# Scan layer of a four-layer convolution network: dt summed on TensorE, one PSUM tile for both banks, wider state rows

## The chip, the cores and the metric

One core of a Trainium2 chip runs the whole program in one launch. The metric is the device time of an execution in microseconds (us). The engines are named as in the profile: PE is TensorE (PEld its weight loads), DVE is VectorE, ACT is ScalarE, POOL is GpSimd, SP is SyncE, which here only issues DMAs. Each engine works through its own queue in order and waits for the others by semaphores.

## What is computed

Four layers, each with a residual: attention blocks on a 3 x 256 x 48 x 48 input, a convolution with weights mixed per image, a plain convolution, and a state-space scan over the 2304 positions of each image. Only the scan layer is touched. Its core in the reference:

```
u = silu(causal_conv(x_in))                       # 512 channels
dt = softplus(dt_raw @ dt_proj_w.T + dt_proj_b)   # 512 channels
def step(hst, inp):
    dt_t, B_t, C_t, u_t = inp
    dA = exp(dt_t[:, :, None] * A)
    hst = hst * dA + dt_t[:, :, None] * B_t[:, None, :] * u_t[:, :, None]
    y_t = einsum('bdn,bn->bd', hst, C_t)          # 16 states per channel
    return hst, y_t
y = (ys + u * D_param) * silu(z)
out = einsum('bld,cd->blc', y, out_proj_w)
```

softplus(p) is computed as max(p, 0) + ln(1 + exp(-|p|)).

## The kernel before

The scan layer cuts each image into 6 chunks of 384 positions, so there are 18 chunks. A chunk has 8 steps (`s`): 4 groups of 128 channels (`m`) times 2 halves of the 16 states (`h`). A step holds a state tile `hs` of 128 partitions x 2 x 4 rows; a row holds one starting state and 384 positions, so 385 columns. Three buffers of `hs` and two of the product `hc` rotate.

In each step:

- `fill` (L1711 on DVE, L1715 on POOL) writes dt·u·B into `hs`, half of the rows by each engine; it is issued one step ahead.
- `decay` (L1740, ACT) writes exp(dt·A) of one row into one of three PSUM slots `ps_da`. It is issued three rows ahead, and a slot is free again when the scan of three rows earlier has ended.
- `scan` (L1748, DVE) runs the recurrence along one row in place. There are 8 per step ("row 0" to "row 7" here).
- `times_c` (L1765, POOL) multiplies the finished tile by C; `add_states` (L1777, L1782, PE) sums the states into `ps_y`; every second step `gate` (L1789, DVE) multiplies by silu(z).

Beside the scans of a chunk, the next chunk is prepared in two PSUM banks, `bank[0]` and `bank[1]` (`ps_g`), which are two tiles. The list `plan` (with `after` and `gating`) fixes where: an entry has a half step `j` (0 to 15, two to a step) and a place in it. MID comes after the second row of the half step, DONE after the third, LATE after the fourth, and PE_ after the fourth too (for odd `j` at the end of the step). `keep_order` makes the order of PE, DVE, ACT and POOL exactly that of the code. The entries that matter:

- `taps` (L1264, PE, j = 0, 1, 3, 4): the causal convolution of one channel group into bank m % 2; `take_u` (L1273, ACT, MID of j = 2, 3, 5, 6) copies each out.
- `project_y` (L1353 and L1355, PE, j = 5 and 6) and `store` (L1365, ACT): the layer's output of the chunk before, in bank 0 and then bank 1.
- `silu` of u (ACT, LATE of j = 7), `project_u` (L1284, PE), `take_dbc` (L1292, ACT, LATE of j = 8), `project_dt` (L1310, PE, j = 8 and 10): the projection p for two channel groups at a time, one per bank.
- `softplus` (ACT, LATE of j = 9 and 11): |p| from each bank (L1319), then exp (L1320) and ln (L1321) on both.
- `take_dt` (DVE, MID of j = 10 and 12): L1326 adds max(p, 0) to the logarithm in the bank, L1327 multiplies dt by u; twice, once per bank.
- `keep_dt` (L1331, ACT, DONE of j = 10 and 12): copies dt out of both banks; DMAs then write dt and dt·u to DRAM, from where `spread` loads them again with each channel repeated.
- `less_mean` (L1222, PE, j = 12), `centre` (L1235 to L1237, ACT), `square_mean` (L1229, PE), `inverse_root` (L1241, L1242, ACT, MID of j = 14), `normalise` (L1246, DVE, MID of j = 15): the layer norm of the chunk after next.
- `project_z` (L1341, PE, j = 13, 14, 15) and `take_z` (L1349, ACT): the gate's input.

Chunk 0 is prepared by `early_preparation` beside the convolution before. In the profile's names, `x`, `u` and `sz` stand for rooms cut out of tiles of other layers that are free by then (dt is one of them), and `wconv` for a piece of a buffer of weights that is free by then.

Of the kernel before, what the change touches and what calls it, by code (L numbers as in the profile page):

```python
# [9 lines left out]
F32 = mybir.dt.float32  # L10
I32 = mybir.dt.int32
AF = mybir.ActivationFunctionType
ALU = mybir.AluOpType
# [3 lines left out]
P = 128  # L17
# [3 lines left out]
CT = 2  # L21
# [4 lines left out]
CH = 384  # L26
# [10 lines left out]
DS = 16  # L37
DTR = 16
DCONV = 4


SUM_MIN, SUM_MAX = 1e-18, 1e18
# [41 lines left out]
def net(  # L84
# [21 lines left out]
    nc = tc.nc  # L106
# [1096 lines left out]
        pass  # L1203


    bank = [psg.tile([P, 512], F32, name=f"ps_g{j}")[:, :CH] for j in range(2)]

# [21 lines left out]
            )  # L1231

    def centre(k):
        for ct in range(CT):
            nc.scalar.copy(k.xg[:, ct, :], bank[ct])  # L1235
        k.sq = room(k, "sq")
        nc.scalar.activation(k.sq, k.xg, AF.Square)  # L1237

# [68 lines left out]
    def project_dt(k, m0):  # L1307
        for j in range(2):
# [3 lines left out]
                start=True, stop=True,  # L1312
            )

    def softplus(k, m0):

        both = k.dt[:, m0 : m0 + 2, :]
        for j in range(2):
            nc.scalar.activation(k.dt[:, m0 + j, :], bank[j], AF.Abs)  # L1319
        nc.scalar.activation(both, both, AF.Exp, scale=-1.0)  # L1320
        nc.scalar.activation(both, both, AF.Ln, bias=1.0)  # L1321

    def take_dt(k, m0):
        for j in range(2):
            m, pdt = m0 + j, bank[j]
            nc.vector.scalar_tensor_tensor(pdt, pdt, 0.0, k.dt[:, m, :], ALU.max, ALU.add)  # L1326
            nc.vector.tensor_tensor(k.dtu[:, m, :], pdt, k.u[:, m, :], ALU.mult)  # L1327

    def keep_dt(k, m0):
        for j in range(2):  # L1330
            nc.scalar.copy(k.dt[:, m0 + j, :], bank[j])  # L1331
        if m0 == 0:
            k.dtd, k.dtud = {}, {}
        d = k.dtd[m0] = dram.tile([P, 2, CH], F32, name=f"dtd{m0}")
        nc.sync.dma_start(d, k.dt[:, m0 : m0 + 2, :])
        d = k.dtud[m0] = dram.tile([P // 2, 2, CH], F32, name=f"dtud{m0}")
        nc.sync.dma_start(d, k.dtu[P // 2 :, m0 : m0 + 2, :])

# [25 lines left out]
    def store(k, mo):  # L1364
# [25 lines left out]
        (7, PE_, 1, project_u),  # L1390
        (8, LATE, 1, take_dbc),
        (8, PE_, 1, lambda k: project_dt(k, 0)),
        (9, LATE, 1, lambda k: softplus(k, 0)),
        (10, MID, 1, lambda k: take_dt(k, 0)),
        (10, DONE, 1, lambda k: keep_dt(k, 0)),
        (10, PE_, 1, lambda k: project_dt(k, 2)),
        (11, LATE, 1, lambda k: softplus(k, 2)),
        (12, MID, 1, lambda k: take_dt(k, 2)),
        (12, DONE, 1, lambda k: keep_dt(k, 2)),
    ]  # L1400

    after = [
# [25 lines left out]
    def early_preparation():  # L1428

        while (2, 1) not in stored:  # L1430
            yield
        fetch(0)
        winx, cwb = x2_rooms()
        k = chunks[0]
        yield
        while 2 not in norm3:
            yield
        group_scale(k)
        yield
        for tap in (0, 1):  # L1440
            fold_taps(winx, cwb, tap)
        less_mean(k)
        yield
        centre(k)
        yield
        square_mean(k)
        yield
        for tap in (2, 3):
            fold_taps(winx, cwb, tap)
        inverse_root(k)  # L1450
        yield
        normalise(k)
        tokens(k)
        fetch(1)
        yield
        for m in (0, 1):
            taps(k, m, 0, 4)
            yield
        take_u(k, 0)
        take_u(k, 1)  # L1460
        yield
        for m in (2, 3):
            taps(k, m, 0, 4)
            yield
        take_u(k, 2)
        take_u(k, 3)
        nc.scalar.activation(k.u, k.u, AF.Silu)
        yield
        k = chunks[1]
        for stage in (group_scale, less_mean, centre, square_mean, inverse_root, normalise):  # L1470
            stage(k)
            yield
        tokens(k)
        yield

        k = chunks[0]
        while 1 not in norm3 or (1, 1) not in stored:
            yield
        x1_rooms()
        yield  # L1480
        project_u(k)
        yield
        take_dbc(k)
        yield
        for m in (0, 2):
            project_dt(k, m)
            yield
            softplus(k, m)
            yield
            take_dt(k, m)  # L1490
            yield
            keep_dt(k, m)
            yield
        for m in (0, 2):
            for j in range(2):
                project_z(k, m + j, j)
            yield
            for j in range(2):
                take_z(k, m + j, j)
            yield  # L1500
# [155 lines left out]
    with ExitStack() as l3:  # L1656
# [48 lines left out]
        def fill(s):  # L1705

            at, m, h = steps[s]
            k = chunks[at]
            hs = tiles[s]
            bb = k.bc[0][:, 2 * h : 2 * h + 2, :].unsqueeze(2).broadcast_to([P, 2, 2, CH])  # L1710
            nc.vector.tensor_tensor(  # L1711
                hs[:, :, 0:2, 1:],
                k.ps[:, :, :CH].unsqueeze(1).broadcast_to([P, 2, 2, CH]), bb, ALU.mult,
            )
            nc.gpsimd.tensor_tensor(  # L1715
                hs[:, :, 2:4, 1:],
                k.rows[m][1].unsqueeze(1).broadcast_to([P, 2, 2, CH]), bb, ALU.mult,
            )

        def first_states(s):  # L1720
            at, m, h = steps[s]
            src = zero if chunks[at].c == 0 else state[m, h]
            hs = tiles[s] = scn.tile([P, 2, 4, CH + 1], F32, name="hs", bufs=3)
            nc.scalar.copy(hs[:, :, :, 0], src.rearrange("p (g q) -> p g q", g=2))

        def last_states(s):
            at, m, h = steps[s]
            if chunks[at].c < NCH - 1:
                t = state[m, h] = wp.tile([P, 8], F32, name=f"hst{m}{h}")
                nc.scalar.copy(t.rearrange("p (g q) -> p g q", g=2), tiles[s][:, :, :, CH])  # L1730

        def decay(n):

# [10 lines left out]

        def scan(s, part):
            g, q = parts_of_step[part]
            b = tiles[s][:, g, q, :]
            nc.vector.tensor_tensor_scan(  # L1748
                b, slots[(8 * s + part) % 3][:, : CH + 1], b, 0.0, ALU.mult, ALU.add
            )  # L1750

        def times_c(s):
            at, m, h = steps[s]
            cb = chunks[at].bc[1][:, 2 * h : 2 * h + 2, :].unsqueeze(2)
            hc = scn.tile([P, 2, 4, CH], F32, name="hc")
            if s == len(steps) - 1:

                for g in range(2):
                    nc.vector.tensor_tensor(
                        hc[:, g], tiles[s][:, g, :, 1:],  # L1760
                        cb[:, g].broadcast_to([P, 4, CH]), ALU.mult,
                    )
                tiles[s] = hc
                return
            nc.gpsimd.tensor_tensor(  # L1765
                hc, tiles[s][:, :, :, 1:], cb.broadcast_to([P, 2, 4, CH]), ALU.mult
            )
            tiles[s] = hc

# [189 lines left out]
```

## Time and profile before

| what | value |
|---|---|
| time, median of 3 runs | 3457.79 us (3455.21 to 3458.74) |
| the profiled execution's own time | 3459.61 us |
| its span | 3458.2 us |
| first and last start of a scan | 2027.6 and 3436.0 us |
| DVE busy over the span | 2940.7 us (85%) |
| POOL busy over the span | 1430.7 us (41%) |
| ACT busy over the span | 2351.8 us (68%) |
| PE busy over the span | 3125.3 us (90%) |

The profile shows one execution. Its groups read "line engine operation out<-in xcount | busy us, mean ns of one | idle us before, and what ended it". In the answers in order of time a row gives start, duration, engine and line, and in brackets the idle time just before it with what ended it; equal neighbours are merged ("x16"), and then the duration is that of all together. One fp32 matmul of 384 columns appears as two records.

### The profile page before, as it was taken

How to read it: one execution, taken by the hardware profiler on the slowest of the kernel's cores; microseconds unless marked ns; L12 is line 12 of the kernel's file. 1: busy time of each engine (PE TensorE's matmuls, PEld its weight loads, DVE VectorE, ACT ScalarE, POOL GpSimd, SP SyncE). 2: the span in 40 equal slices, each digit the busy share in tenths (PEclk: the TensorE clock that was granted, in tenths of full speed). 3: DMA queues.
4: the chain of work that ended last, by engine and by line, in shares of the span. 5: the costliest groups of instructions: out<-in, count | busy, mean ns of one | idle time of the engine just before them, and what ended most of it. 6: DMA issues, size and time to landing. Idle time of an engine off the chain costs nothing.

```text
span 3458.2 us, 51943 instructions
## 1 busy us (share of the span) xinstructions
PE 3125.3 (90%) x20170; PEld 1499.8 (43%) x20170; DVE 2940.7 (85%) x3234; ACT 2351.8 (68%) x3508; POOL 1430.7 (41%) x385
## 2 busy tenths in 40 slices
PE   7999999999999999879999988888888888888885
PEld 4334343443433335447777743333343443333331
DVE  4799899859899994579965379999999999999998
ACT  3788888748888884422224457777777777777774
POOL 0000000000000001110000059999999999999997
PEclk9999999999999999989999989889999999988987
DMA  4000000010000003746402134445444444444441
GB/s 178 14 8 10 8 10 8 8 42 6 10 6 8 10 8 112 249 170 224 139 21 68 46 97 109 115 100 118 116 105 110 106 107 114 116 117 106 117 111 43
DMA packets 167603, 273.95 MB, mean 79 GB/s; under 512 B 30049, under 2 KB 134561, under 8 KB 165426
## 3 DMA queue, kind: packets, MB, share of 16 engines
q1 hardware_dynamic: 154114, 250.48, 26.9%
q10 hardware_dynamic: 13232, 20.06, 1.8%
q8 instruction: 160, 2.62, 0.3%
q14 instruction: 97, 0.79, 0.1%
HBM read 223.12 MB, written 47.10 MB: 78 GB/s over the span
## 4 chain that ended last, share of the span: by engine, by line
PE 54%; DVE 32%; ACT 8%; DMA 3%; issue 2%; POOL 0%; SPq 0%; DVEq 0%; ACTq 0%; POOLq 0%
DVE hs L1748 21%; PE ps_s L637 16%; PE acc L650 14%; PE ps_c L1513 8%; DVE hs L1711 4%; PE ps_g L1222 2%; PE ps_s L1030 2%; ACT ps_da L1740 2%; PE ps_y L461 2%; PE ps_m L664 1%; DVE u L295 1%; PE ps_m L710 1%; ACT L1278 1%; ACT L228 1%; PE acc L528 1%
## 5 line engine op out<-in xcount | busy, mean ns | idle before, releaser
L1748 DVE TENSOR_TENSOR_SCAN hs<-ps_da,hs 128x385 f32<-128x385 f32 x1152 | 1005.6, 938 | 54.4 <-ACT ps_da L1740 35.6
L641 ACT ACTIVATE pt<-ps_s 128x1024 f32<-128x1024 f32 x972 | 942.4, 1022 | 154.8 <-PE ps_s L637 142.2
L856 DVE TENSOR_TENSOR part<-part,pt 128x2048 f32<-128x2048 f32 x396 | 906.6, 2289 | 41.3 <-ACT pt L641 18.5
L1740 ACT ACTIVATE ps_da<-dtr,u 128x384 f32<-128x384 f32 x1152 | 656.0, 582 | 271.3 <-DVE hs L1748 248.4
L163 POOL TENSOR_TENSOR rstd<-ve,mhalf 128x2 f32<-128x2 f32 (+1 forms) x26 | 16.3, 629 | 1477.0 <-DVE ve L161 1477.0
L637 PE MATMUL ps_s<-q,kt 32*128 32x512 f32 (+1 forms) x4320 | 576.4, 592 | 0.1
L650 PE MATMUL acc<-pt,vt 128*32 128x512 f32 (+1 forms) x4320 | 520.9, 561 | 0.2
L1765 POOL TENSOR_TENSOR hc<-hs,x 128x3072 f32<-128x3072 f32 x72 | 446.3, 6198 | 19.8 <-DVE hs L1748 16.5
L1513 PE MATMUL ps_c<-vt,u 128*128 128x288 f32 x1728 | 433.9, 412 | 21.0 <-DVE u L262 21.0
L1765 POOL TENSOR_TENSOR hc<-hs,bc 128x3072 f32<-128x3072 f32 x71 | 438.8, 6181 | 18.6 <-DVE hs L1748 17.2
L1264 PE MATMUL ps_g<-u 128*128 128x384 f32 x1152 | 387.7, 491 | 8.2 <-ACT sz L1349 3.5
L1513 PEld LDWEIGHTS ps_c<-vt,u 128*128 128x128 f32 x1728 | 331.8, 193 | 117.8 <-issue 19.3
L1264 PEld LDWEIGHTS ps_g<-u 128*128 128x128 f32 x1152 | 214.4, 190 | 180.6 <-ACT ps_da L1740 18.7
L637 PEld LDWEIGHTS ps_s<-q,kt 32*128 32x128 f32 x4320 | 195.3, 183 | 199.1 <-issue 120.2
L1782 PE MATMUL ps_y<-hc,u 128*32 128x384 f32 x2304 | 244.8, 548 | 13.8 <-POOL hc L1765 13.8
L1715 POOL TENSOR_TENSOR hs<-dtur,x 128x1536 f32<-128x1536 f32 x72 | 248.4, 3450 | 6.9 <-DMA dtur<-dtud 6.9
L1715 POOL TENSOR_TENSOR hs<-dtur,bc 128x1536 f32<-128x1536 f32 x72 | 249.5, 3465 | 0.0
L650 PEld LDWEIGHTS acc<-pt,vt 128*32 128x32 f32 x4320 | 94.4, 108 | 353.4 <-issue 326.7
L1310 PE MATMUL ps_g<-wconv,u 17*128 17x384 f32 x144 | 79.2, 684 | 82.8 <-ACT x L1331 82.8
L1782 PEld LDWEIGHTS ps_y<-hc,u 128*32 128x32 f32 x2304 | 64.4, 117 | 172.4 <-issue 151.6
L321 POOL MEMSET xpad<- 128x212 f32 x12 | 5.6, 468 | 313.0 <-ACT xpad L1564 234.5
L1529 ACT COPY cb<-ps_c 128x288 f32<-128x288 f32 x48 | 19.2, 400 | 162.9 <-PE ps_c L1513 145.1
(246 smaller groups left out, 3685.3 us busy)
## 6 DMA issues: line engine op xcount, KB each, us to landing
wconv<-in_we SPq DMA_DIRECT2D x144, 384.0 KB, 4.3
dtr<-dtd SPq DMA_DIRECT2D x288, 192.0 KB, 3.9
dtur<-dtud SPq DMA_DIRECT2D x288, 96.0 KB, 4.2
wconv<-xd SPq DMA_DIRECT2D x36, 384.0 KB, 4.3
x<-bcd SPq DMA_DIRECT2D x72, 192.0 KB, 5.7
dtd<-x SPq DMA_DIRECT2D x36, 384.0 KB, 2.9
bc<-bcd SPq DMA_DIRECT2D x72, 192.0 KB, 6.1
yc<-ycat ACTq DMA_DIRECT2D x18, 576.0 KB, 5.0
```

What stands on the lines that cost most here:

```text
L637: nc.tensor.matmul(s[:, j, cols], kt[r, mt * P : (mt + 1) * P], q[r, :n], start=True, stop=True,)
L641: nc.scalar.activation(p[:, h0 : h0 + 2, :], s, AF.Exp)
L650: nc.tensor.matmul(acc[h * HD : (h + 1) * HD, :n], vt[:, mt, g * P + h * HD : g * P + (h + 1) * HD], p[:, h, cols], start=mt == 0, stop=mt ...
L856: ): nc.vector.tensor_tensor(part, first, p, ALU.add)
L1264: nc.tensor.matmul(bank[m % 2], w3v["wtap"][:, tap, ct, m * P : (m + 1) * P], k.xn[:, ct, tap : tap + CH], start=tap == 0 and ct == 0, sto ...
L1513: nc.tensor.matmul(pc[:, :HN], u[:, i, dy, ct, m * P : (m + 1) * P], vt[:, i, ct, dy * TW : dy * TW + HN], start=ct == 0 and dy == 0, stop ...
L1711: nc.vector.tensor_tensor(hs[:, :, 0:2, 1:], k.ps[:, :, :CH].unsqueeze(1).broadcast_to([P, 2, 2, CH]), bb, ALU.mult,)
L1715: nc.gpsimd.tensor_tensor(hs[:, :, 2:4, 1:], k.rows[m][1].unsqueeze(1).broadcast_to([P, 2, 2, CH]), bb, ALU.mult,)
L1740: nc.scalar.activation(slots[n % 3][:, 1 : CH + 1], chunks[at].rows[m][0][:, q, :], AF.Exp, scale=amat[:, col : col + 1],)
L1748: nc.vector.tensor_tensor_scan(b, slots[(8 * s + part) % 3][:, : CH + 1], b, 0.0, ALU.mult, ALU.add)
L1765: nc.gpsimd.tensor_tensor(hc, tiles[s][:, :, :, 1:], cb.broadcast_to([P, 2, 4, CH]), ALU.mult)
L1782: nc.tensor.matmul(k.y_ps[32 * q : 32 * q + 32, :CH], fold, hc[:, g, q, :], start=False, stop=h == 1 and g == 1,)
```

## The change

There are five edits, all in the scan layer.

- The two banks become two halves of one PSUM tile, `banks`; `bank[j]` is a slice of it.
- `centre`, |p| and `keep_dt` handle both banks with one instruction of 768 columns each instead of two of 384.
- |p| moves out of `softplus` to a new entry `positive_part` at MID of j = 9 and 11. The same entry writes max(p, 0) of both banks to the other half of dt's room.
- `sum_dt` at PE_ of j = 9 and 11 multiplies the positive part and the logarithm by the identity into the banks, so PE adds them. `take_dt` becomes one multiplication by u and moves from MID to DONE; `keep_dt` moves from DONE to LATE.
- A row of `hs` has 400 columns: the starting state is in column 15, and the 384 positions begin at column 16.

```diff
+ROW = 16
-    bank = [psg.tile([P, 512], F32, name=f"ps_g{j}")[:, :CH] for j in range(2)]
+    banks = psg.tile([P, 2, 512], F32, name="ps_g")[:, :, :CH]
+    bank = [banks[:, j, :] for j in range(2)]
...
     def centre(k):
-        for ct in range(CT):
-            nc.scalar.copy(k.xg[:, ct, :], bank[ct])
+        nc.scalar.copy(k.xg, banks)
...
+    def pair_of(k, m0):
+        return k.dt[:, m0 : m0 + 2, :]
+
+    def positive_part(k, m0):
+
+        nc.scalar.activation(pair_of(k, m0), banks, AF.Abs)
+        nc.scalar.activation(pair_of(k, 2 - m0), banks, AF.Relu)
+
     def softplus(k, m0):
 
-        both = k.dt[:, m0 : m0 + 2, :]
-        for j in range(2):
-            nc.scalar.activation(k.dt[:, m0 + j, :], bank[j], AF.Abs)
+        both = pair_of(k, m0)
         nc.scalar.activation(both, both, AF.Exp, scale=-1.0)
         nc.scalar.activation(both, both, AF.Ln, bias=1.0)
 
+    def sum_dt(k, m0):
+
+        for part in (2 - m0, m0):
+            for j in range(2):
+                nc.tensor.matmul(
+                    bank[j], ident, k.dt[:, part + j, :],
+                    start=part != m0, stop=part == m0,
+                )
+
     def take_dt(k, m0):
-        for j in range(2):
-            m, pdt = m0 + j, bank[j]
-            nc.vector.scalar_tensor_tensor(pdt, pdt, 0.0, k.dt[:, m, :], ALU.max, ALU.add)
-            nc.vector.tensor_tensor(k.dtu[:, m, :], pdt, k.u[:, m, :], ALU.mult)
+        nc.vector.tensor_tensor(
+            k.dtu[:, m0 : m0 + 2, :], banks, k.u[:, m0 : m0 + 2, :], ALU.mult
+        )
 
     def keep_dt(k, m0):
-        for j in range(2):
-            nc.scalar.copy(k.dt[:, m0 + j, :], bank[j])
+        nc.scalar.copy(pair_of(k, m0), banks)
...
+        (9, MID, 1, lambda k: positive_part(k, 0)),
         (9, LATE, 1, lambda k: softplus(k, 0)),
-        (10, MID, 1, lambda k: take_dt(k, 0)),
-        (10, DONE, 1, lambda k: keep_dt(k, 0)),
+        (9, PE_, 1, lambda k: sum_dt(k, 0)),
+        (10, DONE, 1, lambda k: take_dt(k, 0)),
+        (10, LATE, 1, lambda k: keep_dt(k, 0)),
         (10, PE_, 1, lambda k: project_dt(k, 2)),
+        (11, MID, 1, lambda k: positive_part(k, 2)),
         (11, LATE, 1, lambda k: softplus(k, 2)),
-        (12, MID, 1, lambda k: take_dt(k, 2)),
-        (12, DONE, 1, lambda k: keep_dt(k, 2)),
+        (11, PE_, 1, lambda k: sum_dt(k, 2)),
+        (12, DONE, 1, lambda k: take_dt(k, 2)),
+        (12, LATE, 1, lambda k: keep_dt(k, 2)),
...
-                hs[:, :, 0:2, 1:],
+                hs[:, :, 0:2, ROW:],
...
-            hs = tiles[s] = scn.tile([P, 2, 4, CH + 1], F32, name="hs", bufs=3)
-            nc.scalar.copy(hs[:, :, :, 0], src.rearrange("p (g q) -> p g q", g=2))
+            hs = tiles[s] = scn.tile([P, 2, 4, ROW + CH], F32, name="hs", bufs=3)
+            nc.scalar.copy(hs[:, :, :, ROW - 1], src.rearrange("p (g q) -> p g q", g=2))
...
-            b = tiles[s][:, g, q, :]
+            b = tiles[s][:, g, q, ROW - 1 :]
...
-                hc, tiles[s][:, :, :, 1:], cb.broadcast_to([P, 2, 4, CH]), ALU.mult
+                hc, tiles[s][:, :, :, ROW:], cb.broadcast_to([P, 2, 4, CH]), ALU.mult
```

`early_preparation` gets the same two new stages for chunk 0, and `last_states` reads the last column of the wider row.

More of the change, by code (lines that the diff above doesn't have):

```diff
@@ L1334, in keep_dt @@
         d = k.dtd[m0] = dram.tile([P, 2, CH], F32, name=f"dtd{m0}")
-        nc.sync.dma_start(d, k.dt[:, m0 : m0 + 2, :])
+        nc.sync.dma_start(d, pair_of(k, m0))
         d = k.dtud[m0] = dram.tile([P // 2, 2, CH], F32, name=f"dtud{m0}")
@@ L1487, in early_preparation @@
             yield
+            positive_part(k, m)
             softplus(k, m)
+            yield
+            sum_dt(k, m)
             yield
@@ L1715, in fill @@
             nc.gpsimd.tensor_tensor(
-                hs[:, :, 2:4, 1:],
+                hs[:, :, 2:4, ROW:],
                 k.rows[m][1].unsqueeze(1).broadcast_to([P, 2, 2, CH]), bb, ALU.mult,
@@ L1729, in last_states @@
                 t = state[m, h] = wp.tile([P, 8], F32, name=f"hst{m}{h}")
-                nc.scalar.copy(t.rearrange("p (g q) -> p g q", g=2), tiles[s][:, :, :, CH])
+                nc.scalar.copy(t.rearrange("p (g q) -> p g q", g=2), tiles[s][:, :, :, ROW + CH - 1])
         def decay(n):
@@ L1759, in times_c @@
                     nc.vector.tensor_tensor(
-                        hc[:, g], tiles[s][:, g, :, 1:],
+                        hc[:, g], tiles[s][:, g, :, ROW:],
                         cb[:, g].broadcast_to([P, 4, CH]), ALU.mult,
```

## The prediction

> **What bounds the kernel now.** The change touches the scan layer alone, so I read the windows of 200 us inside it, then the longest waits there, then the groups and one chunk in order of time.
>
> ```profile
> 2100.00:2300.00 200.00, 174.18 (x729) 81.45 (x728) 191.21 (x214) 154.71 (x301) 193.77 (x41) 0.92 0.42 101
> 2300.00:2500.00 200.00, 165.97 (x699) 74.76 (x697) 192.00 (x219) 157.11 (x298) 194.45 (x43) 0.88 0.48 116
> ```
>
> The columns are the length, the busy us of PE, PEld, DVE, ACT and POOL, then granted clock, DMA share and GB/s. DVE (96%) and POOL (97%) are both almost full; either could be the bound.
>
> ```profile
> POOL hc L1765 <- DVE hs L1748: 32.5, 30, 1.6
> DVE hs L1748 <- ACT ps_da L1740: 30.7, 46, 1.5
> ```
>
> From 2100 to 3300 POOL waits for DVE's scans (30 times, 32.5 us), while DVE's largest wait is for ACT's decays, 30.7 us. DVE is thus last, POOL just behind, and ACT can hold DVE up.
>
> One chunk runs from 2269.56 to 2348.46 us, 78.90 us. Starts of its steps (first scans) give the steps' lengths: 8.67, 9.12, 9.35, 9.12, 9.35, 11.26, 10.79, 11.24. POOL's two products take 9.54 a step back to back, 76.3 a chunk: the least a chunk can take without a faster POOL. Below, t counts from 2269.56, and S5 is the start of step 5, and so on (steps are counted from 0). Scans follow each other every 0.854 us.
>
> **DVE's saving.** In steps 5 and 6 the four instructions of take_dt hold the scans up from 2316.90 to 2319.01, 2.11 us.
>
> ```profile
> L1326 DVE SCALAR_TENSOR_TENSOR ps_g<-ps_g,x 128x384 f32<-128x384 f32 x72 | 39.4, 549 | 8.6 <-ACT x L1321 8.6
> L1327 DVE TENSOR_TENSOR dtu<-ps_g,u 128x384 f32<-128x384 f32 x36 | 20.1, 558 | 1.2
> L1246 DVE TENSOR_TENSOR wconv<-wconv,ps_g 128x768 f32<-128x768 f32 x17 | 15.8, 929 | 0.0
> ```
>
> The new multiplication is like L1246 (768 columns, one operand in PSUM): 0.85 from start to start. Saved 2.11 - 0.85 = 1.26, twice a chunk: 2.5 us, 43 us over 17 prepared chunks. At worst it costs two of L1327 (1.1), saving 2.0 a chunk.
>
> **Banks as one tile.** The built program of the change carries its waits, and there every reader or writer of `bank[0]` now also waits for what went before in `bank[1]`, and the other way round. ACT is in order, so a copy that waits for the wrong bank holds back the decays behind it; DVE needs them at most three rows later. PE in the old chunk:
>
> ```profile
> 2272.46 10.59 PE L1264 MATMUL ps_g<-u 128*128 128x384 f32 x32 [0.42 <-ACT sz L1349]
> ...
> 2285.25 5.43 PE L1264 MATMUL ps_g<-u 128*128 128x384 f32 x16
> ...
> 2292.68 5.43 PE L1264 MATMUL ps_g<-u 128*128 128x384 f32 x16
> 2297.95 0.81 PE L1353 MATMUL ps_g<-wconv,ident 128*128 128x384 f32 x2
> 2298.59 2.74 PE L1355 MATMUL ps_g<-x,u 128*128 128x384 f32 x8
> ```
>
> and the copies take_u of groups 0, 2 and 3 on ACT:
>
> ```profile
> 2280.59 0.56 ACT L1273 ACTIVATE x<-ps_g,vec 128x384 f32<-128x384 f32 x1
> ...
> 2293.80 0.56 ACT L1273 ACTIVATE x<-ps_g,vec 128x384 f32<-128x384 f32 x1
> ...
> 2299.07 0.56 ACT L1273 ACTIVATE x<-ps_g,vec 128x384 f32<-128x384 f32 x1
> ```
>
> Each copy runs while PE fills the other bank. With the new waits:
>
> - Step 1: taps(0) waits for the second take_z, 0.37 later than the first, so its start moves from t = 2.90 to 3.27, and taps(0) and (1) end at 3.27 + 10.59 = 13.86. take_u(0), at 11.03 before, starts at 13.9; the decay behind it starts 0.47 later and takes 0.58, to 14.95. Row 5 of step 1 is due at 8.67 + 5 x 0.854 = 12.94: **2.06 us** lost.
> - Step 3: taps(2) now waits for take_u(1), which moves with DVE to t = 17.05. From its start to taps(3)'s is 7.43, and 5.43 more to the end: 29.95. take_u(2), due at 24.24 + 2.06 = 26.3, waits for it; its decay ends at 31.05, where row 1 of step 3 was due at 30.05: **1.05**. take_u(3) waits for project_y(0), 3.35 long, after taps(3) and take_u(2): 33.95, decay at 35.0, row 5 due at 34.52: **0.53**.
> - Step 4: store(1) waits for project_u (2309.9 instead of 2309.47); some 0.1 reaches DVE.
> - Step 7 comes below, since it also depends on the new order.
>
> Unless the copies reach ACT later than I reckon, none of this has cover.
>
> **The sum on PE, and the longer chain.** Costs by rows: |p| over 768 columns 0.80 (the 478 ns of L1319 plus 384 columns at (1485 - 844) / 768 = 0.83 ns, from L1278 and L1320; bounds 0.84 of L1320 and 0.96 for two of L1319), max(p, 0) 0.69 more behind it, exp and ln 0.88 + 0.84, two decays between 1.02, and two fp32 matmuls 1.55 (four records of L1310). ACT has about +0.8 us a chunk net, hidden in the 23% of its time that is idle above; PE has eight matmuls more, 8 x 0.66 = 5.3, hidden in its holes of 4.91 and 3.22 (below); without these covers each would count in full. It is the chain that counts. Step 5: project_dt ends at S5 - 1.71 (2313.46), so the sum ends at S5 - 1.71 + 0.69 + 0.80 + 1.02 + 1.72 + 1.55 = S5 + 4.07. take_dt is reached after three rows, S5 + 2.56: it waits 1.5 and the scans queue behind it. Against the 1.26 saved: +0.25. Step 6 is much the same; there max(p, 0) also waits until the DMA of the first half of dt, 2.9 us in the table of DMA issues, has left the room that it overwrites (the copy's end + 2.9, where ACT would be there after 2.2: 0.7, in front of two decays): a wait of some 1.3 on DVE, net 0. keep_dt moves too: its copy ends some 1.0 later, and with it the stores on SP's queue, behind which stand the loads of L1681. Those were issued at 2333.08, 11 us after, and first read by a decay at about 2346, so I take 0; without that gap the next chunk's first decay would be late by the same 1.0.
>
> Step 7: three rows 2.56, the wait 1.3, take_dt 0.85, a row 0.93, a decay 0.58 and the copy 0.80: keep_dt ends at S6 + 7.0 and less_mean starts there; eight records take 2.85 (L1341) at full clock. centre needs both banks; copy 0.8, square 0.88, square_mean 1.5, project_z(0) 1.45 end at S6 + 14.5 = S7 + 3.7. inverse_root now waits for project_z(0) also. Behind it two more ACT operations and the decay: row 5 runs at S7 + 5.85 instead of 4.27, 1.55 lost (1.14 before). normalise on DVE waits for project_z(1): 3.7, 2.3 for the PE work between, 1.56 itself, 7.55, against row 5's end at 6.75: 0.85. Together 2.4 against 1.14: **+1.26**.
>
> **State rows.** The 1152 scans now start at eight row offsets, 4 bytes apart modulo 64; they take 931 to 964 ns, median 934. So I see no price of alignment on DVE, and take 0. For POOL no row shows an aligned reader of this shape; a gain there is worth 0 (POOL isn't last), a loss is hidden up to 3% now and 10% in the longer chunk.
>
> **Sum.** A chunk: 2.06 + 1.05 + 0.53 + 0.1 + 0.25 + 0 = 4.0, over 17 chunks 68; step 7, 16 x 1.26 = 20. Chunk 0's eight sum matmuls lie in the convolution, 8 x 0.66 = 5.3 if nothing covers them, 0 if all; I take 2.7. Together +91 on 3459.6, the profiled execution; it stands 1.8 above the median: **3548.5**.
>
> **The clock, and two rules.** The clock first, as the trace has it:
>
> ```profile
> 2321.04 2.92 PE L1310 MATMUL ps_g<-wconv,u 17*128 17x384 f32 x4 [4.91 <-ACT x L1331]
> ...
> 2332.30 5.09 PE L1222 MATMUL ps_g<-wconv,u 128*128 128x384 f32 x8 [3.22 <-ACT x L1331]
> ```
>
> After 4.91 us without work the granted clock is 0.50 from 2320 to 2335; L1310 takes 2.92 instead of 1.55 and L1222 5.09 instead of 2.85. The idle times of 0.4 to 0.8 elsewhere in the chunk leave the clock alone. The new sums fill the large hole; the longest gap that I reckon, from project_dt's end to the second sums, is 2.3. It lies between these rows, so the clock costs between 0 and the cold rival's 83 us; being nearer to the small ones, I took full clock. The Trainium skill, "TensorE: Matmul & The Clock Gate", Part 1, puts the fall after an idle window of about 3.4 us: by it 2.3 costs 0. The Trainium skill's "ScalarE: Activation LUTs", Rules for kernel authors, speaks against this change: relu and add belong on VectorE. By it the sum would go without DVE's 43 us of saving, and the rows of L1326 and L1327 are what this trace has for that price.
>
> **The rivals.**
>
> - Faster: the waits for the other bank find slack, and the sum is ready in time. The point: taps(1) ends within 0.8 of take_u(0) reaching ACT (I have 2.8), take_dt waits under 1.26. Then 43 us are saved, and POOL's floor of 76.3 lets 2.6 of a chunk go: 3458 - 43 = 3415. For it: DVE is last and loses work. Against it: the rows above.
> - Cold clock: PE's new gaps still halve the clock in steps 5 to 7. The two final pairs of matmuls cost 1.3 more each and less_mean 2.24: 4.9 a chunk, 83 more, 3631. For it: the clock stayed at 0.5 through 2321 to 2332 although PE worked; against it: the hole that starts it is filled.
> - The stalls and the saving cancel: 3458. It needs the waits of steps 1 and 3 to cost half and the sum to be in time.
>
> **How the numbers follow.** Forecast 0.74, with a range of its own from 3495 (two thirds of the 91, and the sum in time in one of steps 5 and 6, 17 x 1.5 = 25 less) to 3610 (three quarters of the cold clock's price); cold clock 0.13, half of it under 3620; faster 0.10; cancelled 0.03. The range 3495 to 3620 leaves out 0.2. Chances: faster 0.10, same 0.03, slower 0.87, where the same is within 0.2%, about what a measurement of this kernel can tell.
>
> **What would show it.** Right: ACT idle before take_u for PE, some 2.8 us in step 1 and 3.7 in step 3; DVE idle for ps_da of about 6 us a chunk instead of 2; take_dt and normalise idle for PE; a chunk of 84 us; POOL waiting in most steps; clock near 1 in steps 5 to 7. Wrong: a chunk under 78.9, POOL back to back, or hs instructions of POOL or DVE with other durations.

## The result, and the profile after

The changed kernel takes 3581.1 us (median of 4 runs, 3579.69 to 3586.26), the kernel before 3458.26 (4 runs, 3455.21 to 3460.85): a ratio of 1.0358, 95% interval 1.034 to 1.0376. The profiled execution took 3580.79 us, its span 3579.1, 120.9 more than before.

The same two windows, and six lines of the same list of waits from 2100 to 3300 us, of the changed kernel:

```profile
2100.00:2300.00 200.00, 166.09 (x692) 77.43 (x685) 174.00 (x186) 142.94 (x272) 187.20 (x38) 0.95 0.40 98
2300.00:2500.00 200.00, 167.77 (x714) 78.84 (x712) 173.53 (x187) 144.10 (x267) 191.93 (x40) 0.97 0.41 100
```

```profile
DVE hs L1769 <- ACT ps_da L1761: 86.8, 86, 2.0
POOL hc L1786 <- DVE hs L1769: 63.6, 43, 2.4
ACT x L1274 <- PE ps_g L1265: 45.4, 14, 3.7
ACT u L1274 <- PE ps_g L1265: 45.1, 14, 3.6
DVE dtu L1340 <- PE ps_g L1334: 25.7, 14, 2.7
DVE x L1340 <- PE ps_g L1334: 24.2, 14, 2.7
```

DVE fell from 96 to 87%: it has less to do and waits more, 86.8 us for decays (30.7 before) and 49.9 us in a place that is new, take_dt's wait for the sum. ACT, which makes the decays, waits 90.5 us in take_u for the taps. POOL waits twice as long as before (63.6 instead of 32.5) and is still busy 94 to 96%: its instructions became longer.

To find where the time came from I took the start of DVE's fill in each step; the differences are the steps' lengths. The scan stage begins at the same time (first fill 2025.0 before, 2024.9 after). Chunk 0 takes 91.55 us instead of 85.25 (+6.3), the next 15 take 85.33 instead of 78.54 (+6.79, 101.9 in all), the last but one 82.51 instead of 76.78 (+5.7), the last and what follows it 100.2 instead of 93.0 (+7.2). The sum is 121.1. By steps, as a mean over those 15 chunks:

| step | before | after | difference | predicted |
|---|---|---|---|---|
| 1 | 9.11 | 11.19 | 2.08 | 2.06 |
| 3 | 9.11 | 10.94 | 1.83 | 1.05 + 0.53 |
| 4 | 9.35 | 9.53 | 0.18 | 0.1 |
| 5 | 11.24 | 11.76 | 0.52 | 0.25 |
| 6 | 10.81 | 11.51 | 0.70 | 0 |
| 7 | 10.90 | 12.38 | 1.48 | 1.26 |

Steps 0 and 2 did not change. Step 1 and step 3 in one chunk of the changed kernel, first PE, then ACT, then DVE, in order of time:

```profile
2293.04 10.59 PE L1265 MATMUL ps_g<-u 128*128 128x384 f32 x32 [1.71 <-ACT sz L1363]
2306.89 5.43 PE L1265 MATMUL ps_g<-u 128*128 128x384 f32 x16 [0.99 <-ACT x L1274]
2314.32 5.43 PE L1265 MATMUL ps_g<-u 128*128 128x384 f32 x16
```

```profile
2303.67 0.58 ACT L1274 ACTIVATE x<-ps_g,vec 128x384 f32<-128x384 f32 x1 [2.80 <-PE ps_g L1265]
...
2319.79 0.58 ACT L1274 ACTIVATE x<-ps_g,vec 128x384 f32<-128x384 f32 x1 [3.64 <-PE ps_g L1265]
2323.95 0.58 ACT L1274 ACTIVATE x<-ps_g,vec 128x384 f32<-128x384 f32 x1 [1.50 <-PE ps_g L1369]
```

```profile
2304.76 2.66 DVE L1769 TENSOR_TENSOR_SCAN hs<-ps_da,hs 128x385 f32<-128x385 f32 x3 [1.96 <-ACT ps_da L1761]
...
2320.88 3.51 DVE L1769 TENSOR_TENSOR_SCAN hs<-ps_da,hs 128x385 f32<-128x385 f32 x4 [0.94 <-ACT ps_da L1761]
2325.04 2.66 DVE L1769 TENSOR_TENSOR_SCAN hs<-ps_da,hs 128x385 f32<-128x385 f32 x3 [0.66 <-ACT ps_da L1761]
```

Take_u(0) no longer runs beside the taps of the other bank: it starts at 2303.67, when all 32 records have ended (2293.04 + 10.59 = 2303.63), and ACT has then been idle for 2.80 us. Of that, 1.96 reaches DVE, as the decay behind it comes late. In step 3 it is the same with taps(3) (3.64 and 0.94) and then with project_y (1.50 and 0.66).

### The profile page after: what moved, and what is told of

Read it like the earlier page. It is cut to its first block, busy times and chain, and to the rows that moved or that the text cites. A ratio compares the mean times of both kernels' runs of the same rounds, so it can differ in the third digit from the quotient of the medians.

```text
span 3579.1 us, 52385 instructions
## 1 busy us (share of the span) xinstructions
PE 3200.6 (89%) x20458; PEld 1540.7 (43%) x20458; DVE 2911.8 (81%) x3126; ACT 2357.7 (66%) x3454; POOL 1510.8 (42%) x385
## 5 line engine op out<-in xcount | busy, mean ns | idle before, releaser
L1761 ACT ACTIVATE ps_da<-dtr,u 128x384 f32<-128x384 f32 x1152 | 647.5, 580 | 223.3 <-DVE hs L1769 212.6
L1786 POOL TENSOR_TENSOR hc<-hs,x 128x3072 f32<-128x3072 f32 x72 | 485.5, 6743 | 42.2 <-DVE hs L1769 38.0
L1786 POOL TENSOR_TENSOR hc<-hs,bc 128x3072 f32<-128x3072 f32 x71 | 478.2, 6735 | 34.4 <-DVE hs L1769 34.4
L651 PEld LDWEIGHTS acc<-pt,vt 128*32 128x32 f32 x4320 | 94.4, 108 | 353.4 <-issue 326.7
L1803 PE MATMUL ps_y<-hc,u 128*32 128x384 f32 x2304 | 225.1, 510 | 21.9 <-POOL hc L1786 20.9
L1334 PE MATMUL ps_g<-x,ident 128*128 128x384 f32 x288 | 156.9, 698 | 73.2 <-ACT x L1322 58.4
L1334 PEld LDWEIGHTS ps_g<-x,ident 128*128 128x128 f32 x288 | 68.2, 261 | 155.7 <-ACT x L1322 80.5
```

Source lines behind the costliest of these rows:

```text
L651: nc.tensor.matmul(acc[h * HD : (h + 1) * HD, :n], vt[:, mt, g * P + h * HD : g * P + (h + 1) * HD], p[:, h, cols], start=mt == 0, stop=mt ...
L1334: nc.tensor.matmul(bank[j], ident, k.dt[:, part + j, :], start=part != m0, stop=part == m0,)
L1761: nc.scalar.activation(slots[n % 3][:, 1 : CH + 1], chunks[at].rows[m][0][:, q, :], AF.Exp, scale=amat[:, col : col + 1],)
L1786: nc.gpsimd.tensor_tensor(hc, tiles[s][:, :, :, ROW:], cb.broadcast_to([P, 2, 4, CH]), ALU.mult)
L1803: nc.tensor.matmul(k.y_ps[32 * q : 32 * q + 32, :CH], fold, hc[:, g, q, :], start=False, stop=h == 1 and g == 1,)
```

## Experiments

In the expectations W stands for the theory that the waits for the other bank, which one PSUM tile brings, are the main cost; P for the rival that the new rows slow POOL, so that POOL becomes the bound; L for the rival that the longer chain to dt is the cost. All times in the table are us; "product" is POOL's product in ns, between the means of its two groups from 2100 to 3300 us; the ratio is to the kernel before in the same runs. The lengths are those of each kernel's one profiled execution. Such an execution leaves chunk 0 uncertain by some 1.5 us: it takes 85.25 us in the kernel before and 83.75 with rows of 401 (below), whose middle chunks agree to 0.04.

| kernel | time | ratio, 95% | chunk 0 | middle | step 5 | step 6 | step 7 | last and tail | product |
|---|---|---|---|---|---|---|---|---|---|
| before | 3458.3 | | 85.25 | 78.54 | 11.24 | 10.81 | 10.90 | 93.0 | 6189 |
| after | 3581.1 | 1.034 to 1.038 | 91.55 | 85.33 | 11.76 | 11.51 | 12.38 | 100.2 | 6739 |
| one tile alone | 3573.3 | 1.032 to 1.036 | 89.63 | 85.33 | 11.37 | 10.93 | 13.35 | 94.1 | 6181 |
| rows of 400 alone | 3499.3 | 1.011 to 1.015 | 83.59 | 80.78 | 11.30 | 10.80 | 10.87 | 101.3 | 6727 |
| sum on PE alone | 3461.5 | 1.000 to 1.002 | 92.19 | 78.27 | 10.91 | 11.59 | 10.18 | 93.3 | 6190 |
| whole, two tiles | 3512.1 | 1.015 to 1.018 | 89.28 | 80.63 | 11.73 | 11.19 | 10.21 | 102.5 | 6723 |
| whole, rows of 385 | 3573.8 | 1.031 to 1.034 | 91.84 | 85.36 | 11.94 | 11.36 | 12.38 | 94.4 | 6182 |
| whole, own room | 3582.2 | 1.034 to 1.037 | 90.02 | 85.26 | 11.85 | 11.35 | 12.38 | 100.5 | 6744 |
| sum alone, own room | 3430.9 | 0.991 to 0.994 | 82.62 | 76.79 | 10.92 | 10.09 | 10.19 | 92.8 | 6191 |

### One PSUM tile alone

The kernel before with

```diff
-    bank = [psg.tile([P, 512], F32, name=f"ps_g{j}")[:, :CH] for j in range(2)]
+    banks = psg.tile([P, 2, 512], F32, name="ps_g")[:, :, :CH]
+    bank = [banks[:, j, :] for j in range(2)]
```

> The kernel before, with its two banks as two halves of one PSUM tile and nothing else changed. Theory W (the waits for the other bank are the main cost): take_u in steps 1 and 3, store in step 4, inverse_root and normalise in step 7 wait as in the changed kernel; 2.06 + 1.58 + 0.1 + 1.26 = 5.0 us a chunk more, 17 chunks, about 3543. Theory P (the new rows slow POOL's product with C from 6.19 to 6.74, and POOL is what the changed kernel is short of): POOL is untouched here, so about 3458. Theory L (the longer chain to dt is the cost): about 3458.

3573.3 us. Steps 1 and 3 take 11.19 and 10.94, as in the changed kernel to the hundredth, and the middle chunks the same 85.33, though steps 5 to 7 divide their part otherwise. Theory W was right on the cause and 30 us too low in its 3543, above all in step 7: 2.45 us more than before (13.35 for 10.90), where W had 1.26. This one edit, which adds no instruction, costs 117 us beside the kernel before in the same runs (3456.3), where the whole change costs 123.

### The whole change on two tiles

The changed kernel with the diff above turned round, and one instruction for each bank where the change has one for both:

```diff
-        nc.scalar.activation(pair_of(k, m0), banks, AF.Abs)
+        for j in range(2):
+            nc.scalar.activation(k.dt[:, m0 + j, :], bank[j], AF.Abs)
```

and so for centre, max(p, 0), take_dt and keep_dt.

> The changed kernel with two PSUM tiles for the banks again (so |p|, max(p, 0), the multiplication by u and the copies of dt and of the centred input are two instructions of 384 columns each); the sum on PE and the rows of 400 stay. Theory W: steps 1, 3 and 7 lose their waits, 5.0 of 85.4 us a chunk, but POOL's two products then need 8 x (6.74 + 3.48) = 81.8 us a chunk, less a little overlap, so a chunk of about 81.5 and 3581 - 17 x 3.9 = 3515. Theory P: nothing changes for POOL, about 3575. Theory L: about 3575.

3512.1: the one tile, with the instructions that it joins, is worth 69 us in the changed kernel and not 117, since POOL now stands behind. Its product takes 6.72 us, from 2100 to 3300 us it is idle only once (6.5 us, for a DMA of chunk 0), and a chunk of 80.6 is what it needs.

### Rows of 400 columns alone

```diff
-            hs = tiles[s] = scn.tile([P, 2, 4, CH + 1], F32, name="hs", bufs=3)
+            hs = tiles[s] = scn.tile([P, 2, 4, 400], F32, name="hs", bufs=3)
```

with the positions from column 16, as in the change, on the kernel before.

> The kernel before with the state rows of 400 columns, positions from column 16, and nothing else changed. If POOL's product takes 6.74 here too, the rows are its cause; POOL then needs 81.5 us a chunk against 78.5 before and becomes the bound: 3458 + 17 x 3.0 + 5 for the last chunk = 3514. If the product takes 6.19, the slower POOL in the changed kernel comes from other work beside it: 3458. Theory W would have 3458 in either case but for POOL.

3499.3, 43 us slower. One of its windows, and DVE's longest waits:

```profile
2300.00:2500.00 200.00, 166.79 (x669) 73.58 (x670) 187.49 (x213) 153.45 (x292) 200.00 (x42) 0.85 0.47 111
```

```profile
DVE hs L1748 <- POOL hs L1715: 28.4, 46, 1.4
DVE hs L1748 <- ACT ps_da L1740: 27.3, 44, 1.5
```

POOL is busy all of the 200 us, and DVE's scans wait for POOL's half of the fill, which they did not before. So P is a true mechanism, if a smaller cost. The scans did not change (some 0.94 us).

### The sum on PE alone

The changed kernel on two tiles, as above, and with rows of 385:

```diff
-ROW = 16
+ROW = 1
```

> The changed kernel with two PSUM tiles and with rows of 385 columns: of the change only the sum on PE, the positive part on ACT and the moved stages are left. Theory L: steps 5 and 6 wait for the sum as in the changed kernel (1.3 and 1.9 us), which takes back the saving of 2 x 1.0; step 7 is as before: a chunk of 79.5 to 80, about 3480. If the chain costs nothing once the banks are apart: 2.0 us a chunk saved, 3424. Theory W and theory P: about 3424 to 3458.

3461.5: +5 us, so by itself the sum brings nothing. But that is a balance of gains and losses. Steps 5 and 7 are shorter by 0.33 and 0.72, step 6 is longer by 0.78, and chunk 0 by 6.9. ACT's row for max(p, 0) of the second half in chunk 0, and SP's queue at that time:

```profile
2095.99 0.87 ACT L1324 ACTIVATE x<-ps_g 128x384 f32<-128x384 f32 x2 [7.81 <-DMA dtd<-x]
```

```profile
2084.19 5.01 SPq L1303 DMA_DIRECT2D bc<-bcd  x8
2089.30 0.38 SPq L1351 DMA_DIRECT2D dtd<-x  x1
```

Max(p, 0) overwrites the half of dt that the DMA still has to store, and this DMA stands on SP's queue behind eight loads that take 5.01 us. Its data is ready when the copies of dt end, at 2085.85, and it is issued at 2089.30. It is also the slowest of its line: from issue to landing it takes 6.6 us, where the median of the 36 such stores of this run is 2.4. So of the wait some 3.5 us are the queue's and 4.2 the DMA's own time above the median; why it was slow isn't shown. I had reckoned with this wait, but with 0.7 us, by a DMA of 2.9 us with nothing ahead of it.

### A room of its own for max(p, 0)

The kernel with the sum alone, and max(p, 0) written to a room that is free at that time (`sq`, used for the norm in step 6):

```diff
-            nc.scalar.activation(k.dt[:, 2 - m0 + j, :], bank[j], AF.Relu)
+            nc.scalar.activation(rooms["sq"][0][:, j, :], bank[j], AF.Relu)
...
-        for part in (2 - m0, m0):
+        for n, part in enumerate((rooms["sq"][0], pair_of(k, m0))):
...
```

> This is the sum on PE alone (two PSUM tiles for the banks, rows of 385 columns), with one more edit: max(p, 0) is written to a room that is free at that time, not over the other half of dt, so it no longer waits for the DMA that stores that half. Measured without this edit: 3461.5 us, middle chunks 78.2 us, chunk 0 of the scan stage 92.2 us (85.3 before), where max(p, 0) of the second half waited 7.8 us for that DMA. If the DMA is what makes chunk 0 longer and costs some 0.2 to 0.6 us in the sixth step of the others: chunk 0 at 85 to 86, middle chunks 77.8, 3445 to 3452 us. If the longer chain to dt (the second ln, the sum, and only then the multiplication) is the cost by itself: chunk 0 stays near 92 and the time near 3461.

3430.9 us, ratio 0.9925 (0.9912 to 0.9939): faster than the kernel before by 26 us, and more than I expected. Chunk 0 is 9.6 us shorter, and each middle chunk 1.48, where I had reckoned with 0.2 to 0.6: without this edit ACT waits for that DMA 15 times from 2100 to 3300, 16.6 us in all, and take_dt behind it. What bounds this kernel is POOL; its product's groups from 2100 to 3300:

```profile
L1787 POOL TENSOR_TENSOR hc<-hs,bc 128x3072 f32<-128x3072 f32 x64 | 395.7, 6183 | 5.0 <-DVE hs L1770 4.4
L1787 POOL TENSOR_TENSOR hc<-hs,x 128x3072 f32<-128x3072 f32 x62 | 384.3, 6198 | 0.4 <-DVE hs L1770 0.2
```

It is idle for some 6 of 1200 us. So the sum on PE brings a gain once the other two edits and this wait are away, and the gain ends about where POOL is full. From chunk 3 on, its middle chunks alternate between 77.2 to 77.3 us and 76.3 to 76.4; the difference lies in step 6 and comes below, with the clock.

### take_dt one row later

The kernel with its own room, and both take_dt moved:

```diff
-        (10, DONE, 1, lambda k: take_dt(k, 0)),
+        (10, LATE, 1, lambda k: take_dt(k, 0)),
...
-        (12, DONE, 1, lambda k: take_dt(k, 2)),
+        (12, LATE, 1, lambda k: take_dt(k, 2)),
```

> As the kernel with a room of its own for max(p, 0), and take_dt comes after the fourth row of its half step, not after the third, directly ahead of keep_dt. If DVE's wait for the sum (1.3 to 2.1 us in the changed kernel at this place) is what the longer chain costs, a fourth scan of 0.85 us fills that much of it twice a chunk: middle chunks 76.3 to 77 us (76.3 is what POOL's two products take at 6.19 us), 3420 to 3432 us in all. If the wait only moves on to the copy of dt and the mean of the next chunk's norm behind it (seventh step), the time stays within 5 us of the kernel without this edit.

3429.6 us, the same: 0.9919 (0.9906 to 0.9933). Step 5 becomes 10.29 instead of 10.92 and step 7 11.20 instead of 10.19. DVE's wait for the sum falls from 13.9 to 0.2 us of the 1200, but its wait for decays grows from 17.4 to 33.8, and the chunk stays at 76.76. POOL is idle 6.9 of the 1200 us, 0.44 a chunk, so its own work is 76.3, the floor that I had reckoned, and little was left to gain. Both cases of the expectation allow this time; the waits say that it was the second, in which the wait only moves.

### The whole change with a room of its own

```diff
-        nc.scalar.activation(pair_of(k, 2 - m0), banks, AF.Relu)
+        nc.scalar.activation(rooms["sq"][0][:, 0:2, :], banks, AF.Relu)
...
-        for part in (2 - m0, m0):
+        for n, part in enumerate((rooms["sq"][0], pair_of(k, m0))):
...
```

> The changed kernel (one tile, rows of 400), but max(p, 0) goes to a room of its own, so it doesn't wait for the DMA of the other half of dt. In the changed kernel that wait shows 5 times in 14 chunks, 2.4 us in all, while the sixth step (counted from 0) takes 11.4 to 11.7 us against 10.9 with one tile alone. If the longer chain by itself makes that step longer: 3578 to 3582 us, sixth step unchanged. If the DMA does it: sixth step 10.9 or less, some 0.6 us a chunk, 3567 to 3573 us.

3582.2, no gain: in the changed kernel the chunk is so much longer that the DMA has mostly ended (5 waits, 2.4 us in all). Step 6 takes 11.35, only 0.16 less. So it is hardly the DMA that makes step 6 of the changed kernel longer than before; what does comes below, with the clock.

### The whole change with rows of 385

```diff
-ROW = 16
+ROW = 1
```

> The changed kernel with rows of 385 columns as before, all else of the change kept. The rows alone, on the kernel before, cost 43 us, as POOL's product took 6.72 us and POOL became the bound. If POOL is hidden by the waits of the changed kernel (its middle chunks take 85.4 us, POOL's work 81.8), only the last chunk, which has no preparation beside it and took 65.2 us where it took 62.6 before, and the tail behind it get shorter: 3571 to 3576 us, middle chunks 85 to 85.5. If the parts add up as they were measured alone: 3581 - 43 = 3538 us.

3573.8 us, as reckoned with POOL hidden. The middle chunks stay at 85.36; the last chunk and the tail go back from 100.2 to 94.4. The wider rows cost 43 us alone and 7 here: the longer chunk hides them, except where there is nothing to prepare.

### What in the rows makes POOL slow

Two more kernels, each the kernel before with one change: rows of 400 whose positions begin at column 1, and rows of 401 that begin at column 16. The diffs show two of the places; the fill, the scans and the copies of the states use the same columns.

The first:

```diff
-            hs = tiles[s] = scn.tile([P, 2, 4, CH + 1], F32, name="hs", bufs=3)
+            hs = tiles[s] = scn.tile([P, 2, 4, 400], F32, name="hs", bufs=3)
...
-                hc, tiles[s][:, :, :, 1:], cb.broadcast_to([P, 2, 4, CH]), ALU.mult
+                hc, tiles[s][:, :, :, 1 : 1 + CH], cb.broadcast_to([P, 2, 4, CH]), ALU.mult
```

The second:

```diff
-            hs = tiles[s] = scn.tile([P, 2, 4, CH + 1], F32, name="hs", bufs=3)
+            hs = tiles[s] = scn.tile([P, 2, 4, 401], F32, name="hs", bufs=3)
...
-                hc, tiles[s][:, :, :, 1:], cb.broadcast_to([P, 2, 4, CH]), ALU.mult
+                hc, tiles[s][:, :, :, 16 : 16 + CH], cb.broadcast_to([P, 2, 4, CH]), ALU.mult
```

> The kernel before with rows of 400 columns, but with the positions from column 1 on (starting state in column 0). So the rows' starts lie a multiple of 64 bytes apart, each 4 bytes behind a boundary of 64. Known: rows of 385 from column 1, POOL's product 6.19 us and 3458 us; rows of 400 from column 16, 6.72 us and 3499 us. If the distance of the rows makes POOL slow: 6.7 us and about 3500 us. If a start on the same boundary as the product's two other operands makes it slow: 6.2 us and about 3458 us.

> The kernel before with rows of 401 columns, positions from column 16 on: as wide as the new rows, but each row starts 4 bytes further from a boundary of 64 than the row ahead of it. If it is the width or the larger tile that makes POOL slow: 6.7 us and about 3500 us. If it is the equal place of all rows against a boundary of 64 bytes: 6.2 us and about 3458 us.

3497.9 and 3459.4 us (one run each). POOL's product in the first and in the second, from 2100 to 3300:

```profile
L1765 POOL TENSOR_TENSOR hc<-hs,bc 128x3072 f32<-128x3072 f32 x62 | 415.7, 6704 | 0.0
```

```profile
L1765 POOL TENSOR_TENSOR hc<-hs,bc 128x3072 f32<-128x3072 f32 x64 | 395.7, 6182 | 16.5 <-DVE hs L1748 13.9 <-PE ps_g L1222 2.6
```

Rows 1600 bytes apart make it slow, from whichever column they start (6.70 and 6.73 us); rows 1604 bytes apart do not (6.18), as wide as they are. Of distance, start and width, it is the distance.

Then I tried whether other operands of POOL show the same, on the kernel with its own room: rows of 385 for the spread dt·u that the fill reads, and for the product that POOL writes.

```diff
-            dtur = scn.tile([P, 2, CH], F32, name="dtur")
+            dtur = scn.tile([P, 2, CH + 1], F32, name="dtur")[:, :, :CH]
```

> The kernel with the sum on PE alone and a room of its own for max(p, 0) (3430.9 us, POOL back to back, chunks 76.8 us), with rows of 385 columns for the spread dt.u too, which POOL's fill reads (fill now 3.46 us for 1536 columns, 2.25 ns a column; the product with staggered rows 2.01 ns, with rows a multiple of 64 bytes apart 2.19). If a distance of rows that is a multiple of 64 bytes makes any input of POOL slow: fill some 3.1 to 3.2 us, 2.2 to 2.6 us a chunk off POOL's work, of which DVE, idle about 2 us a chunk, lets some 1 to 2 through: 3400 to 3420 us. If only the product's eight rows show it: 3.46 us and 3431 us.

```diff
-            hc = scn.tile([P, 2, 4, CH], F32, name="hc")
+            hc = scn.tile([P, 2, 4, CH + 1], F32, name="hc")[:, :, :, :CH]
```

> The kernel with the sum on PE alone and a room of its own for max(p, 0) (3430.9 us, POOL idle 6 of 1200 us), with rows of 385 columns for the product that POOL writes (hc) too. Known: rows of 385 instead of 400 in the state tile that the product reads take it from 6.72 to 6.19 us; rows of 385 in the input of POOL's fill change nothing. If the rows' distance counts for what POOL writes as for what it reads: product under 6.1 us, some 0.1 to 0.5 us a step less of POOL's work, 3405 to 3425 us. If only the state tile's rows count: 6.19 us and 3429 to 3433 us.

3429.2 (ratio 0.9904 to 0.9931) and 3429.9 us (0.9912 to 0.9939): neither does anything. The fill of the first, and the product of the second:

```profile
L1737 POOL TENSOR_TENSOR hs<-dtur,bc 128x1536 f32<-128x1536 f32 x64 | 220.8, 3449 | 1.3 <-ACT ps_da L1762 0.8 <-POOL hc L1787 0.2 <-POOL u L1253 0.2
```

```profile
L1787 POOL TENSOR_TENSOR hc<-hs,bc 128x3072 f32<-128x3072 f32 x64 | 395.3, 6176 | 6.2 <-DVE hs L1770 5.7
```

So the effect is known for the eight rows of the state tile that the product reads, and for no other operand here. Why it is so stays open. Rows at another multiple of 64 bytes were not tried.

## Why the prediction was right, and where its sum was off

The forecast was +91 on the profiled execution, the result +121. The main mechanism, the waits for the other bank, and its places were right; 30 us came from terms that were too small. Of the signs named beforehand, two did not show: POOL waited in 43 of 113 steps and not in most, and the clock was not near 1 in steps 5 and 6. One sign of being wrong did show: POOL's product, an instruction on `hs`, took 6.74 us instead of 6.19.

**Waits for the other bank: right.** Steps 1, 3 and 4 came to 2.08, 1.83 and 0.18 for a forecast of 2.06, 1.58 and 0.1, and one tile alone gives the same three steps. The idle times of ACT were foreseen to a tenth (2.8 and 3.7 forecast, 2.80 and 3.64 seen). It could be reckoned, since all of it was the order of the queues and durations that the trace had.

**Step 7: right.** +1.48 for 1.26; the length after, 12.38, was 12.50 in the forecast. The remainder is on the other side: I had taken step 7 of one chunk (11.24) for the old length, and the mean is 10.90. Its two waits, and the mean of the next norm on PE:

```profile
2368.39 0.96 DVE L1769 TENSOR_TENSOR_SCAN hs<-ps_da,hs 128x385 f32<-128x385 f32 x1 [1.48 <-ACT ps_da L1761]
2370.06 0.95 DVE L1247 TENSOR_TENSOR wconv<-wconv,ps_g 128x768 f32<-128x768 f32 x1 [0.71 <-PE ps_g L1355]
```

```profile
2358.80 2.85 PE L1224 MATMUL ps_g<-wconv,u 128*128 128x384 f32 x8 [1.19 <-ACT x L1345]
```

The forecast had 1.55 and 0.85. Less_mean is at full clock, as assumed (2.85 us, 5.09 before). With one tile alone, and so without the sums that fill the hole ahead of it, step 7 takes 13.35.

**Steps 5 and 6: the step that failed is the full clock.** I had +0.25 and 0, and measured +0.52 and +0.70. The forecast had said that the longest gap of 2.3 us lies between the rows of 0.8 and 4.91, and taken the near end. PE around the sums in this chunk, and the clock of some short windows:

```profile
2339.19 1.56 PE L1334 MATMUL ps_g<-x,ident 128*128 128x384 f32 x4 [1.60 <-ACT x L1322]
2341.80 1.56 PE L1334 MATMUL ps_g<-x,ident 128*128 128x384 f32 x4 [1.05 <-ACT x L1328]
...
2346.62 1.97 PE L1311 MATMUL ps_g<-wconv,u 17*128 17x384 f32 x4 [0.99 <-ACT x L1345]
2350.95 4.59 PE L1334 MATMUL ps_g<-x,ident 128*128 128x384 f32 x8 [2.36 <-ACT x L1322]
```

```profile
2344.00:2347.00 3.00, 2.01 (x17) 0.68 (x10) 3.00 (x5) 1.74 (x4) 3.00 (x2) 1.00 1.06 207
2347.00:2348.00 1.00, 1.00 (x4) 0.37 (x2) 1.00 (x2) 0.65 (x3) 1.00 (x1) 0.81 0.68 238
2348.00:2349.00 1.00, 0.59 (x1) 0.00 (x0) 1.00 (x3) 0.37 (x1) 0.57 (x2) 0.50 0.46 169
2350.00:2353.00 3.00, 2.05 (x3) 1.18 (x4) 2.90 (x4) 2.88 (x5) 3.00 (x1) 0.50 0.75 166
```

The first sums ran at full clock, 1.56 us a pair. Behind gaps of 1.60, 1.05 and 0.99 us the clock falls to 0.50 between 2347 and 2348, while project_dt runs (1.97 us instead of 1.55), so ahead of the longest gap and not because of it. The second sums then take 4.59 us instead of 2 x 1.56, and in all 17 prepared chunks of the stage 4.5 us or more. In 12 of the 17 they begin at half clock, behind the same three gaps. In the other 5 the clock had fallen earlier, in the gap of 1.60 ahead of the first sums, so that these ran cold; it came back and fell again during the second sums. What parts the 5 from the 12 is when they come: in the trace's clock records every fall of the stage lies on a grid of 3.413 us (to 0.002), and the first sums of the 5 start 0.68 to 0.94 us after a point of that grid, those of the 12 at 0.97 to 1.81. Take_dt's wait is 2.68 us where the first sums ran cold, and 1.31 in this chunk, where they did not:

```profile
2258.33 0.96 DVE L1340 TENSOR_TENSOR dtu<-ps_g,u 128x768 f32<-128x768 f32 x1 [2.68 <-PE ps_g L1334]
```

```profile
2343.40 0.96 DVE L1340 TENSOR_TENSOR x<-ps_g,x 128x768 f32<-128x768 f32 x1 [1.31 <-PE ps_g L1334]
2355.58 0.96 DVE L1340 TENSOR_TENSOR x<-ps_g,x 128x768 f32<-128x768 f32 x1 [2.08 <-PE ps_g L1334]
```

The difference, 1.37, is one pair at half clock (2.93 against 1.56). In step 6 the wait was 1.3 in the forecast and is 1.8 in the mean of the 17. The forecast's 1.3 held 0.7 for the DMA, which in the changed kernel is mostly absent (5 waits, 2.4 us in all), so the half clock took the place of that term and added 0.5 to it. So the rival of the cold clock came true for one of its two sums, in part for the other, and not for less_mean, which was its dearest part.

The kernel with its own room shows the price of the clock within one run: in 7 of its 17 chunks the last pair of the second sums takes 2.93 us and step 6 takes 10.64, in the other 10 it takes 1.56 to 1.95 and step 6 9.61 to 9.66. One chunk of each kind, first the pair, then the next operation of take_dt:

```profile
2474.51 2.93 PE L1336 MATMUL ps_g<-x,ident 128*128 128x384 f32 x4
2551.93 1.87 PE L1336 MATMUL ps_g<-x,ident 128*128 128x384 f32 x4 [0.28 <-ACT x L1330]
```

```profile
2477.47 0.56 DVE L1342 TENSOR_TENSOR x<-ps_g,x 128x384 f32<-128x384 f32 x1 [0.72 <-PE ps_g L1336]
2553.42 1.00 DVE L1342 TENSOR_TENSOR dtu<-ps_g,u 128x384 f32<-128x384 f32 x2
```

No run kept PE busy in the gaps, so that this would hold the clock up is not shown.

The Trainium skill, "TensorE: Matmul & The Clock Gate", Part 1, says that the clock falls after an idle window of about 3.4 us, and by that the forecast's longest gap of 2.3 cost 0. The rows above show the fall behind gaps none of which is over 1.60 us, and the measurement decides. The same section says that this window runs freely, so that the point of the transition depends on where in the window the first matmul lands; the grid of 3.413 us, and 5 cold first sums of 17 behind the same gaps, agree with that.

**DVE's saving: right in size, given back.** The new take_dt takes 0.96 us with the next scan 0.87 behind its start, for 0.85 forecast. A gain shows in the kernel with two tiles, rows of 385 and its own room, 26 us faster than before, but not all of it is this saving: of the 1.75 us that its middle chunks are shorter, 1.04 lie in steps 5 and 6, and 0.71 in step 7, where less_mean runs at full clock (2.85 us) behind the sums. In the changed kernel it goes into the waits above: with one tile and rows of 385, the sum on PE makes no difference that the runs can tell (3573.8 with it, 3573.3 without).

**State rows: the term taken as 0 was 7.** The reading for DVE was right. For POOL I had bounded the loss by its cover, 3% in the old chunk and 10% in the longer one. The product's loss was 9%, which is 5% of POOL's work (where POOL is the bound a chunk takes 76.8 us with rows of 385 and 80.6 with rows of 400), and in the middle chunks it is hidden as stated. But the last chunk is not longer: there is no preparation beside it and nothing that hides POOL. Its 7.2 us (7.3 by the run with rows of 385) are missing from the sum, which asked for the cover only where the chunk is long.

**Chunk 0: 2.7 forecast for its sums beside the convolution, none seen** (first fill at 2025.0 and 2024.9). But the first fill of the other kernels' profiled executions lies between 2017.0 and 2029.7, also where nothing ahead of it was changed (2017.0 with rows of 400 alone, 2026.7 with rows of 401), so one execution of each can't settle a term of 2.7.

Put together: the middle chunks 15 x (6.79 - 5.26) = 23, the last but one 1.7, chunk 0 about 1 more in its steps, the end 7.2, less 2.7: 30 us.

## What to carry to other kernels

Joining two buffers into one tile can cost more than any instruction that it saves: write down, for each in-order queue, what every reader and writer now waits for, and what stands behind it. When the parts of a change are measured alone, they need not add up (117 + 43 + 5 = 165 here, for 123): a cost on a second engine counts only where the first is not already longer, so look for the stretch without that cover, mostly the last one. And before a new intermediate result goes into a room that a store still reads, look at what is queued ahead of that store, and at the longest and not only the median time that such a store takes to land.

## What the runs showed of the hardware

POOL's product of 3072 columns takes 6.18 to 6.20 us when the state tile's rows lie 1540 or 1604 bytes apart, and 6.70 to 6.74 when they lie 1600 apart, whether they start on a multiple of 64 bytes or 4 bytes behind one. DVE's scans do not show it. PE's clock fell to half behind gaps of 1.60, 1.05 and 0.99 us within 9.1 us, not only in one of 4.91; its falls in the scan stage lie on a grid of 3.413 us, and which matmuls run cold depends on where on it they come.
